# A transformer block with two kinds of attention: the products with the values placed on their own, up to two key tiles in a run

## The chip, the cores and the metric

The kernel runs on one core of a Trainium2 chip. The metric is the device time of one execution in microseconds (us); the lower it is, the better. Engines are named as in the profile: PE is TensorE with its matmuls, PEld its weight loads, DVE is VectorE, ACT is ScalarE, POOL is GpSimd, SP is SyncE, which issues nearly all DMAs here. SBUF is the memory on the core, PSUM the memory that matmuls write, DRAM the memory outside.

## The reference

Eight independent batches of 512 tokens with 256 features pass through four residual layers, all in float32:

```python
x = x + attn_a(layernorm(x))      # 16 heads of 16, latent keys and values, rope, softmax with a distance mask
x = x + ffn(layernorm(x))         # 256 -> 1024, relu, -> 256
x = x + attn_b(layernorm(x))      # one head of 256, no softmax: (q k^T * decay) v
x = x + ffn(layernorm(x))         # the same weights again
# attn_a, cut to its core:
#   q = rope(x Wq + bq);  k, v = split((x Wdown + bdown) Wup + bup);  k = rope(k)
#   att = softmax(q k^T / 4 + mask(distance));   out = att v + 0.2 * sigmoid(q . mean(k)) * mean(v)
#   return out Wo + bo
```

## The kernel before

**The first attention** is cut into items: a batch has four groups of four heads, so there are 32 groups, and a group has eight steps of scores. Score item `n` (`score_item`) holds two heads' scores for one tile of 128 queries against 512 keys; DVE reduces them to row maxima (`reduce_item`, the `mr<-s` of the profile). When a group's eight items are done, the maxima are transposed (`mx`), negated on ACT (`neg`) and sent by a DMA into a spare row of the transposed queries `qT`, so that the second pass of scores comes out with the maximum already subtracted. The second pass (`prob_item`, the `t` of the profile) computes the scores transposed, keys on partitions; ACT takes the exponential into a tile `p` of 128 x 2 x 512 (`soft_item`), and POOL, or DVE where the planner says so, multiplies it by the distance mask, in two halves. The product with the values (`pv_item`) takes two such items, that is four heads and one tile of 128 keys: four matmuls with 32 output columns each, which accumulate over the group's four key tiles into one PSUM bank, `pv`. Each float32 matmul shows as two in the trace. The values carry a column of ones, so that `pv` also holds the sums of the softmax.

After a group's last key tile, the units of `post_units` follow: ACT copies `pv` into `num` (evacuate); then either SP moves `num` into `aT` (numerators, heads on partitions) and `sums`, DVE takes reciprocals, two DMAs spread them through DRAM into `rec`, and DVE divides; or, in groups 2 and 3 of some batches, PE transposes `num` and divides on DVE (`num`, `aT` flips). When a batch's last group is done, `("aT", b)` is given, and the projection `wo` of that batch may begin.

**Everything else** is written as units: layer norms (`st_`, `mv_`, `xn_`, `tr_` for each of the norms a, f, r and g), the latent and rotary fronts (`lat`, `k`, `q`, `v`, `ga`, `me`), `wo`, the hidden layers (`hx`, eight units of four matmuls, then `x`, four units of sixteen), and the second attention (`b`, `bv`, `bs`, `bo`). A unit has an estimated PE time, a list of what other engines do after it, predecessors, and needs.

**The order** on every engine is fixed by the program: the calls are kept in program order, and the function `plan` decides that order. It keeps a clock for each engine and goes through the steps: step `t` issues the scores of item `t` and the second pass of item `t - LAG` (LAG is 12). Between steps it issues units, taking whatever is ready soonest, with a credit that spreads the units over the remaining steps; `posts`, `shifts` and the fronts go ahead of the rest. `plan` is tried with 96 sets of rules, and the set with the lowest planned cost is emitted. After the last step the remaining units follow in the order in which they become ready.

In the kernel before, the values' product belongs to a step. The third entry of a step is `t - LAG - PVLAG` (PVLAG is 3); where that is an odd item, the step begins with one key tile's four matmuls, and then come the scores. Two pairs of banks (`ps_sc`, bufs 2) serve the scores of both passes; three banks (`ps_m`) serve the units; in the early steps the second pass may use those (`spare`). The tiles `p` have four buffers, `num` and `neg` two.

**Loads.** Three buffers hold batches of `x`. The load of batch b + 3 is issued (`fetch`) when the second half of `wo` of batch b has been issued; its DMA then waits, in SP's queue, for DVE's addition that read the old contents. The statistics of the new batch come into DVE's queue from a set step on.

Of the kernel before, what the change touches and what calls it, by code (L numbers as in the profile page):

```python
# [35 lines left out]
def tile_kernel(  # L36
# [47 lines left out]
    ps_m = ctx.enter_context(tc.tile_pool(name="ps_m", bufs=3, space=PSUM))  # L84

    xv = x.rearrange("b (t p) d -> b p t d", p=P)
    ov = out.rearrange("b (t p) d -> b p t d", p=P)
# [32 lines left out]

    wq_in = at.tile([P, NC, NH, 32], F32, tag="p", bufs=4, name="wq_in")

    def load_wq():
        act.dma_start(wq_in.rearrange("p c h d -> p c (h d)"), wq[:, :, 0, :])

    wk_in = at.tile([P, NH, 32], F32, tag="p", bufs=4, name="wk_in")
    move(wk_in.rearrange("p h d -> p (h d)"), wk[:, 0, :].unsqueeze(0).to_broadcast([2, LAT, NH * 32]))
# [126 lines left out]
    NS = 8 * NI  # L254
    LAG, PVLAG = 12, 3
    PER = 8 * NG
# [30 lines left out]
    def bias_rows():  # L287
        move(b_row.rearrange("j (c p) -> p (j c)", p=P), vecs[:, V_BQB : V_BQB + 2 * NC])
        wr["rows"] = at.tile([P, 4, D], F32, tag="p", bufs=4, name="b_rows")
        move(wr["rows"][:, 0:2, :], b_row.unsqueeze(0).to_broadcast([P, 2, D]))  # L290
# [85 lines left out]
    def front1(b):  # L376
# [53 lines left out]
        s, (h0, h1) = ln_units(lambda: xs[b], f"a{b}", fr)  # L430
        free = PER * (b - 1) + LAG + PVLAG + 2
        u = {"lat": Unit(latent, 1720, (("ACT", 700),), after=[h0[2], h1[2]]), "latent": latent}
        u["v"] = Unit(values, 950, (("ACT", 1350),), after=[u["lat"]], step=free, bank=2)
        u["mv"] = Unit(mean_v, 250, (("DVE", 250), ("POOL", 1400)), after=[u["lat"]])
# [14 lines left out]
    def front2(b, u1):  # L449
# [18 lines left out]
        def half_unit(j, e, ps, order="cs"):  # L468
            for n in order:
                table = cos if n == "c" else nsin  # L470
                if b == 0 and (j, e) == (0, 1):
                    if not spare:
                        spare["t"] = at.tile([P, 2, T], F32, tag="p", bufs=4, name="rq1_0")
# [26 lines left out]
        def mean_k():  # L500
            m = fr.tile([P, 2], F32, tag="mk", name=f"mk_{b}")
            for e in range(2):
                unused = fr.tile([P, T], F32, tag="unused", name=f"unused{e}_{b}")
                act.activation(unused, rot[1, e], AF.Identity, accum_out=m[:, e : e + 1])
                gps.tensor_scalar(kmean[:, e, :NH], hmask, m[:, e : e + 1], None, ALU.mult)
# [6 lines left out]

        free = PER * (b - 1) + LAG + PVLAG + 2
        lat = u1["lat"]
# [70 lines left out]
    def soft_item(n, ps):  # L585
        i, r = divmod(n, 8)
        t, pair = r // 2, 1 - r % 2
        p = at.tile([P, 2, T], F32, tag="p", bufs=4, name=f"p_{n}")
        if spare[n]:
            for e in range(2):  # L590
                act.activation(p[:, e, :], ps[e], AF.Exp, scale=0.25)
        else:
            act.activation(p, ps[2], AF.Exp, scale=0.25)
        o = (NT - 1 - t) * P
        eng = gps if pooled[n] else dve
        for e in range(2):
            eng.tensor_tensor(p[:, e, :], p[:, e, :], late["dec_a"][:, o : o + T], ALU.mult)
        probs[(i, t, pair)] = p
# [21 lines left out]
    def post_units_dma(i):  # L620
        b, g = divmod(i, NG)
        c = g // 2

        def evacuate():
            num = at.tile([P, T], F32, tag="num", name=f"num_{i}")
            act.copy(num, pv[i])
            if g == 0:
                aT[b] = at.tile([P, NC, T], F32, tag="aT", name=f"aT_{b}")
            if g % 2 == 0:
                sums[c] = at.tile([P, 2, HD], F32, tag="sums", name=f"sums_{b}_{c}")  # L630
            move(sums[c][:, g % 2, :], num[HD:P:32])
# [13 lines left out]

        def divide():
            dve.tensor_mul(aT[b][:, c, :], aT[b][:, c, :], sums["rows", c])

        u = [Unit(evacuate, then=(("ACT", 600), (None, 7500)))]
        if g % 2:  # L650
            u.append(Unit(invert, then=(("DVE", 350), (None, 12000)), after=u[-1:]))
            u.append(Unit(divide, then=(("DVE", 700),), after=u[-1:], gives=("aT", b) if g == NG - 1 else None))
        return u

    def post_units(i, fast):
# [5 lines left out]
        def evacuate():  # L661
            num = at.tile([P, T], F32, tag="num", name=f"num_{i}")
            act.copy(num, pv[i])
            s["num"] = num
# [29 lines left out]
    def rest(b):  # L694
# [27 lines left out]
        def ffn(norm, src, dst, last):  # L722
# [3 lines left out]
            def up(f):  # L726
                if b == B - 1:
                    if f == 0:
                        s["h"] = []
                    if f % 2 == 0:  # L730
                        s["h"].append(at.tile([P, 2 * T], F32, tag="p", bufs=4, name=f"h_{dst}_{f}"))
                elif f == 0:
# [22 lines left out]
        def keys(o):  # L755
            if o == 0:
                s["v"], s["w"] = [], []
                if b == B - 1:
                    p = [at.tile([P, 2 * T], F32, tag="p", bufs=4, name=f"ret_{j}") for j in range(4)]
                    room = [(p[1], 0), (p[1], D + 1), (p[1], 2 * D + 2), (p[3], 0)]  # L760
# [140 lines left out]
    def plan(reserve, later, early, fast, lead, bias, emit=False):  # L901
# [5 lines left out]
        banks = deque([0, 0, 0])  # L907
        given = {("wo", -2), ("wo", -1), ("x", 1), ("x1", -1)}
# [66 lines left out]

        def values_of(t):
            n = steps[t][2]
            return n if n > 0 and n % 2 == 1 else None

        def step_start(t):  # L980

            s, ts, _ = steps[t]
            n = values_of(t)
            at_ = clock["PE"]
            if n is not None:
                at_ = max(at_, prob_at[n] - 100, prob_at[n - 1] - 100)
            own = 0
# [14 lines left out]
            own = both  # L1002
            return max(at_, own - (1000 if n is not None else 0))

        def step(t):
            s, ts, _ = steps[t]
            at_ = step_start(t)
# [9 lines left out]
            shape[0] = "S"  # L1017
            n = values_of(t)
            if n is not None:
                if emit:  # L1020
                    pv_item(n)
                at_ += 1000
                if n % 8 == 7:
                    us = post_units(n // 8, fast)
                    made = Unit(None)
                    made.done = at_ + 100
                    us[0].after.append(made)
                    posts.extend(us)
            if s is not None or ts:
                at_ += 1070  # L1030
            clock["PE"] = at_
# [45 lines left out]

        gaps, shape, landed = [], ["S"], {}
        shifts, posts = [], []
        setup = [Unit(lambda: xs.update({2: load_x(2)}), step=20, gives=("x", 2))]  # L1080
# [33 lines left out]
        t, credit, share = LAG, 0, 0  # L1114
        while t < LAST or any(chains) or posts or shifts:
            while True:
# [15 lines left out]
            for rank, c in enumerate([shifts, posts] + chains):  # L1132
# [19 lines left out]
            if take and best is None:  # L1152

                able = [c for c in [shifts, posts] + chains if c and c[0].step <= t and start_of(c[0]) is not None]
                if not able:
# [129 lines left out]
```

## Time and profile before

| | |
|---|---|
| time, median of 3 runs | 1297.86 us (1295.99 to 1302.39) |
| the profiled execution | 1296.18 us, span 1294.3 us |
| mean granted TensorE clock | 0.987 |
| matmuls and weight loads in the trace | 6110 each |
| multiplications of `p` by the mask, POOL | 472 halves, 597.5 us |
| the same, DVE | 40 halves, 41.5 us |
| exponentials of 128 x 1024, ACT | 229, mean 1.02 us |

The page of the profile gives busy times by engine, the chain of work that ended last, and groups of instructions (line, engine, operation, names, count, busy time, mean time, and the idle time ahead of them with what ended it). Nearly all instructions stand on two lines, 69 and 201, because helpers issue them; so one goes by names. A name such as `x` can be several tiles (the input, and the results of layers, whose buffer numbers are left out). The trace can be asked for the order of a stretch, for the chain of waits in it and for busy times and granted clock in it.

### The profile page before, as it was taken

The page shows a single profiled execution, that of the slowest core. Times are in us where ns is not written, and L with a number is a line of the kernel's source. Part 1 is how long each engine was busy: PE and PEld are TensorE (multiplying, and loading weights), DVE is VectorE, ACT ScalarE, POOL GpSimd, SP SyncE. Part 2 cuts the span into 40 slices and gives each one's busy share as a digit, 9 for nine tenths or more (in the row PEclk, how much of TensorE's full clock was granted, in tenths as well). Part 3 has the DMA queues.
Part 4 walks back from the last instruction along what each step waited for, and adds up shares of the span by engine and source line. Part 5 has one row for each costly group of instructions (what it writes and reads, how often), then busy time and mean ns, then how long its engine had stood idle before and what let it go on. Part 6 is the DMA issues. An engine that isn't in the chain of part 4 may idle for free.

```text
span 1294.3 us, 15776 instructions
## 1 busy us (share of the span) xinstructions
PE 1235.9 (95%) x6110; PEld 618.5 (48%) x6110; DVE 654.4 (51%) x979; ACT 456.7 (35%) x655; POOL 768.0 (59%) x753
## 2 busy tenths in 40 slices
PE   7999899899999999999999999999999999998998
PEld 5423344244444543445534544445544464575675
DVE  4777665758443675444755267452644354313130
ACT  2245343443434334342243323432343424312201
POOL 4389866787576767765577555783567645602010
PEclk9999999999999999999999989999999999998999
DMA  5301010001000100010000100010000000000000
GB/s 138 126 20 32 9 48 5 10 17 39 9 22 11 45 5 14 5 51 30 14 6 22 38 25 14 6 40 29 12 2 10 18 13 14 1 17 1 1 16 17
DMA packets 30870, 30.80 MB, mean 24 GB/s; under 512 B 12721, under 2 KB 22194, under 8 KB 30516
## 3 DMA queue, kind: packets, MB, share of 16 engines
q1 hardware_dynamic: 29884, 29.01, 8.1%
q8 instruction: 48, 0.79, 0.3%
q10 hardware_dynamic: 912, 0.79, 0.2%
q14 instruction: 26, 0.21, 0.1%
HBM read 13.39 MB, written 4.39 MB: 14 GB/s over the span
## 4 chain that ended last, share of the span: by engine, by line
PE 82%; DVE 12%; DMA 2%; issue 2%; POOL 1%; ACT 1%; SPq 0%; ACTq 0%; DVEq 0%
PE s L201 18%; PE hx L201 17%; PE x L201 17%; DVE mr L69 6%; PE pv L201 5%; PE wo L201 3%; PE bs L201 3%; PE bo L201 3%; PE t L201 2%; PE b L201 2%; PE q L201 2%; PE bv L201 2%; DVE xn_a L69 1%; PE warm L201 1%; PE lat L201 1%
## 5 line engine op out<-in xcount | busy, mean ns | idle before, releaser
L69 POOL TENSOR_TENSOR p<-p,dec_a 128x512 f32<-128x512 f32 x472 | 597.5, 1289 | 265.6 <-ACT p L69 263.2
L69 DVE TENSOR_REDUCE mr<-s 128x2 f32<-128x1024 f32 x256 | 312.5, 1222 | 286.1 <-PE t L201 252.8
L69 ACT ACTIVATE p<-t 128x1024 f32<-128x1024 f32 (+1 forms) x283 | 263.2, 942 | 494.0 <-PE t L201 476.0
L201 PE MATMUL s<-kT,qT 32*128 32x512 f32 x1024 | 290.6, 643 | 26.1 <-DVE mr L69 25.6
L201 PE MATMUL t<-qT,kT 32*128 32x512 f32 x1024 | 290.6, 645 | 2.6 <-DVE mv_a L69 1.6
L201 PE MATMUL x<-w_sb,h_x 128*128 128x256 f32 x1024 | 233.6, 383 | 0.0
L201 PEld LDWEIGHTS x<-w_sb,h_x 128*128 128x128 f32 x1024 | 191.2, 190 | 54.7 <-issue 30.1
L201 PEld LDWEIGHTS s<-kT,qT 32*128 32x128 f32 x1024 | 78.0, 184 | 191.7 <-DVE mr L69 96.3
L201 PE MATMUL pv<-p,va 128*32 128x512 f32 x1024 | 141.6, 619 | 0.0
L69 DVE TENSOR_TENSOR x<-x,x 128x256 f32<-128x256 f32 x64 | 27.2, 424 | 218.9 <-PE x L201 218.9
L69 ACT ACTIVATE h_x<-hx,vec 128x512 f32<-128x512 f32 x128 | 88.0, 687 | 133.2 <-PE hx L201 129.1
L201 PE MATMUL hx<-xT_g,w_sb 128*128 128x512 f32 x256 | 119.5, 614 | 2.0 <-ACT xT_g L69 2.0
L201 PE MATMUL hx<-xT_f,w_sb 128*128 128x512 f32 x256 | 118.7, 602 | 0.8 <-ACT xT_f L69 0.8
L201 PEld LDWEIGHTS t<-qT,kT 32*128 32x128 f32 x1024 | 78.7, 185 | 17.9 <-ACT p L69 5.4
L201 PEld LDWEIGHTS hx<-xT_g,w_sb 128*128 128x128 f32 x256 | 47.8, 195 | 65.6 <-issue 59.1
L201 PEld LDWEIGHTS hx<-xT_f,w_sb 128*128 128x128 f32 x256 | 45.7, 190 | 61.7 <-issue 55.4
L69 POOL TENSOR_TENSOR x<-x,b 128x256 f32<-128x256 f32 x64 | 48.1, 771 | 15.4 <-DVE xn_g L69 8.0
L201 PEld LDWEIGHTS pv<-p,va 128*32 128x32 f32 x1024 | 21.2, 109 | 73.8 <-issue 51.5
L69 POOL TENSOR_SCALAR ve_g<-mv_g 128x2 f32<-128x2 f32 x16 | 3.5, 219 | 85.4 <-DVE mv_g L69 85.4
L69 DVE TENSOR_TENSOR p<-p,dec_a 128x512 f32<-128x512 f32 x40 | 41.5, 1078 | 7.3 <-ACT p L69 7.1
L69 POOL TENSOR_TENSOR rc<-rc,rs 128x512 f32<-128x512 f32 x30 | 39.2, 1329 | 9.1 <-DVE rs L69 9.1
L201 PE MATMUL bs<-xT_r,ret 128*128 128x512 f32 (+3 forms) x128 | 38.3, 441 | 0.0
(144 smaller groups left out, 1068.4 us busy)
## 6 DMA issues: line engine op xcount, KB each, us to landing
kT<-rc SPq DMA_DIRECT2D x64, 64.0 KB
out_dram<-x SPq DMA_DIRECT2D x32, 128.0 KB
qT<-rc SPq DMA_DIRECT2D x60, 64.0 KB
x<-in_x_dram SPq DMA_DIRECT2D x7, 512.0 KB
aT<-num SPq DMA_DIRECT2D x96, 32.0 KB
rec<-d_rec SPq DMA_DIRECT2D x12, 256.0 KB
w_sb<-in_w_dram SPq DMA_DIRECT2D x2, 1024.0 KB
x<-in_x_dram SPq DMA_DIRECT2D x2, 256.0 KB
```

Source lines behind the costliest of these rows:

```text
L69: ins = f(*a, **k)
L201: tc.keep_in_program_order(nc.tensor.matmul(o, lhsT=l, rhs=r, start=start, stop=stop))
```

## The change

The product with the values is taken out of the steps and becomes a thing of its own. A counter `valued[0]` says how many items have been consumed. `values_start(k)` gives the planned time at which the next `k` key tiles (one or two, of the same group) could start: PE's clock, the planned end of the multiplications of their items less 100 ns, and, for a group's first tile, the evacuation of the group before. `values(k)` emits them, and after a group's last tile it makes the units of `post_units`. In the loop, rules decide when: where the buffers of `p` would run out, or after the last step, products go at once (two if the second is soon ready); else two go when both are ready and the last thing issued was a unit, or when the next step is more than 1700 ns away and no unit can start; else one goes when the wait is over 300 ns (FILL) and no unit can start. If a unit could start and the last thing was a step, the unit is issued first. A step thus has only its scores.

The tiles `p` get seven buffers (PB); `num` and `neg` get one each; the mean over the keys writes its unused result into a rotary tile that is no longer needed, in place of a tile of its own. The values' projection of batch b (`u["v"]`) waits for the last product of batch b - 2 by name, where it waited for a step, and the rotary keys' step moves from LAG + PVLAG + 2 to LAG + 1. The 96 sets of rules are as before.

```diff
+    PB = 7
-    LAG, PVLAG = 12, 3
+    LAG, FILL = 12, 300
...
-        free = PER * (b - 1) + LAG + PVLAG + 2
-        u["v"] = Unit(values, 950, (("ACT", 1350),), after=[u["lat"]], step=free, bank=2)
+        u["v"] = Unit(values, 950, (("ACT", 1350),), after=[u["lat"]], needs=(("pv", b - 2),), bank=2)
...
-                unused = fr.tile([P, T], F32, tag="unused", name=f"unused{e}_{b}")
-                act.activation(unused, rot[1, e], AF.Identity, accum_out=m[:, e : e + 1])
+                act.activation(rot["s", 1, e], rot[1, e], AF.Identity, accum_out=m[:, e : e + 1])
...
-        free = PER * (b - 1) + LAG + PVLAG + 2
+        free = PER * (b - 1) + LAG + 1
...
-        neg = at.tile([NG * NT, P], F32, tag="neg", name=f"neg_{i}")
+        neg = at.tile([NG * NT, P], F32, tag="neg", bufs=1, name=f"neg_{i}")
...
-        p = at.tile([P, 2, T], F32, tag="p", bufs=4, name=f"p_{n}")
+        p = at.tile([P, 2, T], F32, tag="p", bufs=PB, name=f"p_{n}")
...
-            num = at.tile([P, T], F32, tag="num", name=f"num_{i}")
+            num = at.tile([P, T], F32, tag="num", bufs=1, name=f"num_{i}")
...
-        steps = [(t, [t - LAG] if t >= LAG else [], t - LAG - PVLAG) for t in range(NS)]
-        steps += [(None, [n, n + 1], n - 3) for n in range(NS - LAG, NS, 2)] + [(None, [], NS - 3), (None, [], NS - 1)]
+        steps = [(t, [t - LAG] if t >= LAG else []) for t in range(NS)]
+        steps += [(None, [n, n + 1]) for n in range(NS - LAG, NS, 2)]
...
+        def values_start(k):
+            d, last = valued[0], valued[0] + 2 * k - 1
+            if d >= NS or d % 8 + 2 * k > 8 or last not in prob_at:
+                return None
+            t = max(clock["PE"], *(prob_at[n] - 100 for n in range(d, last + 1)))
+            return max(t, drawn[0]) if d % 8 == 0 else t
+
+        def values(k):
+            s = values_start(k)
+            stands(s - clock["PE"])
+            clock["PE"] = s + (520 if shape[0] == "S" else 130) + 870 * k
+            shape[0] = "V"
+            for _ in range(k):
+                n = valued[0] = valued[0] + 2
+                if emit:
+                    pv_item(n - 1)
+            if n % 8 == 0:
+                us = post_units(n // 8 - 1, fast)
...
+                posts.extend(us)
+                drawn[0] = max(clock["PE"] + 100, clock["ACT"]) + 700
+                if n % PER == 0:
+                    given.add(("pv", n // PER - 1))
...
-            n = values_of(t)
-            if n is not None:
-                if emit:
-                    pv_item(n)
-                at_ += 1000
-                if n % 8 == 7:
-                    us = post_units(n // 8, fast)
...
+            full = t < LAST and steps[t][1] and steps[t][1][-1] - valued[0] >= PB
+            one, two = values_start(1), values_start(2)
+            soon = clock["PE"] + 50
+            wait = (s_step or clock["PE"] + 2500) - clock["PE"]
+            other = best is not None and best[2] <= soon
+            k = 0
+            if full or t >= LAST and one is not None:
+                k = 2 if two is not None and two <= max(one, clock["PE"]) + 400 else 1
+            elif two is not None and two <= soon and (shape[0] == "U" or wait > 1700 and not other):
+                k = 2
+            elif one is not None and one <= soon and wait > FILL and not other:
+                k = 1
+            if k and other and shape[0] == "S":
+                credit -= best[1][0].pe
+                issue(best[1].pop(0))
+                continue
+            if k and (full or t < LAST or values_start(k) <= soon):
+                values(k)
+                continue
```

More of the change, by code (lines that the diff above doesn't have):

```diff
@@ L119, in tile_kernel @@
     move(bd, vecs[:LAT, V_BD : V_BD + 1].unsqueeze(0).to_broadcast([2, LAT, 1]))
-    wq_in = at.tile([P, NC, NH, 32], F32, tag="p", bufs=4, name="wq_in")
+    wq_in = at.tile([P, NC, NH, 32], F32, tag="p", bufs=PB, name="wq_in")
     def load_wq():
         act.dma_start(wq_in.rearrange("p c h d -> p c (h d)"), wq[:, :, 0, :])
-    wk_in = at.tile([P, NH, 32], F32, tag="p", bufs=4, name="wk_in")
+    wk_in = at.tile([P, NH, 32], F32, tag="p", bufs=PB, name="wk_in")
     move(wk_in.rearrange("p h d -> p (h d)"), wk[:, 0, :].unsqueeze(0).to_broadcast([2, LAT, NH * 32]))
@@ L288, in bias_rows @@
         move(b_row.rearrange("j (c p) -> p (j c)", p=P), vecs[:, V_BQB : V_BQB + 2 * NC])
-        wr["rows"] = at.tile([P, 4, D], F32, tag="p", bufs=4, name="b_rows")
+        wr["rows"] = at.tile([P, 4, D], F32, tag="p", bufs=PB, name="b_rows")
         move(wr["rows"][:, 0:2, :], b_row.unsqueeze(0).to_broadcast([P, 2, D]))
@@ L472, in half_unit @@
                     if not spare:
-                        spare["t"] = at.tile([P, 2, T], F32, tag="p", bufs=4, name="rq1_0")
+                        spare["t"] = at.tile([P, 2, T], F32, tag="p", bufs=PB, name="rq1_0")
                     t = spare["t"][:, "cs".index(n), :]
@@ L661, in evacuate @@
         def evacuate():
-            num = at.tile([P, T], F32, tag="num", name=f"num_{i}")
+            num = at.tile([P, T], F32, tag="num", bufs=1, name=f"num_{i}")
             act.copy(num, pv[i])
@@ L730, in up @@
                     if f % 2 == 0:
-                        s["h"].append(at.tile([P, 2 * T], F32, tag="p", bufs=4, name=f"h_{dst}_{f}"))
+                        s["h"].append(at.tile([P, 2 * T], F32, tag="p", bufs=PB, name=f"h_{dst}_{f}"))
                 elif f == 0:
@@ L758, in keys @@
                 if b == B - 1:
-                    p = [at.tile([P, 2 * T], F32, tag="p", bufs=4, name=f"ret_{j}") for j in range(4)]
+                    p = [at.tile([P, 2 * T], F32, tag="p", bufs=PB, name=f"ret_{j}") for j in range(4)]
                     room = [(p[1], 0), (p[1], D + 1), (p[1], 2 * D + 2), (p[3], 0)]
@@ L907, in plan @@
         banks = deque([0, 0, 0])
-        given = {("wo", -2), ("wo", -1), ("x", 1), ("x1", -1)}
+        given = {("wo", -2), ("wo", -1), ("pv", -2), ("pv", -1), ("x", 1), ("x1", -1)}
         held = []
@@ L974, in shift_unit @@
             return u
-        def values_of(t):
-            n = steps[t][2]
-            return n if n > 0 and n % 2 == 1 else None
+        def values_start(k):
[15 more added lines that the diff above has]
+                us = post_units(n // 8 - 1, fast)
+                made = Unit(None)
+                made.done = clock["PE"] + 100
+                us[0].after.append(made)
+                posts.extend(us)
+                drawn[0] = max(clock["PE"] + 100, clock["ACT"]) + 700
+                if n % PER == 0:
+                    given.add(("pv", n // PER - 1))
         def step_start(t):
-            s, ts, _ = steps[t]
-            n = values_of(t)
+            s, ts = steps[t]
             at_ = clock["PE"]
-            if n is not None:
-                at_ = max(at_, prob_at[n] - 100, prob_at[n - 1] - 100)
             own = 0
@@ L1002, in step_start @@
             own = both
-            return max(at_, own - (1000 if n is not None else 0))
+            return max(at_, own)
         def step(t):
-            s, ts, _ = steps[t]
+            s, ts = steps[t]
             at_ = step_start(t)
@@ L1017, in step @@
             shape[0] = "S"
-            n = values_of(t)
-            if n is not None:
-                if emit:
-                    pv_item(n)
-                at_ += 1000
-                if n % 8 == 7:
-                    us = post_units(n // 8, fast)
[L1025 to L1030, printed above, removed]
+            at_ += 1070
             clock["PE"] = at_
@@ L1078, in plan @@
         gaps, shape, landed = [], ["S"], {}
+        valued, drawn = [0], [0]
         shifts, posts = [], []
@@ L1114, in plan @@
         t, credit, share = LAG, 0, 0
-        while t < LAST or any(chains) or posts or shifts:
+        while t < LAST or any(chains) or posts or shifts or valued[0] < NS:
             while True:
@@ L1152, in plan @@
             if take and best is None:
+                if valued[0] < NS:
+                    values(1)
+                    continue
                 able = [c for c in [shifts, posts] + chains if c and c[0].step <= t and start_of(c[0]) is not None]
```

## The prediction

> **What bounds the kernel now.** I read the page first: busy shares and the chain that ended last.
>
> ```profile
> PE 1235.9 (95%) x6110; PEld 618.5 (48%) x6110; DVE 654.4 (51%) x979; ACT 456.7 (35%) x655; POOL 768.0 (59%) x753
> PE 82%; DVE 12%; DMA 2%; issue 2%; POOL 1%; ACT 1%; SPq 0%; ACTq 0%; DVEq 0%
> ...
> L69 DVE TENSOR_REDUCE mr<-s 128x2 f32<-128x1024 f32 x256 | 312.5, 1222 | 286.1 <-PE t L201 252.8
> L201 PE MATMUL pv<-p,va 128*32 128x512 f32 x1024 | 141.6, 619 | 0.0
> ```
>
> PE has 82% of the chain, DVE 12%. The values' products (`pv`) are 1024 matmuls in 128 key tiles of eight, 141.6 us or 1.1 us a tile. Their number does not change, so the question is what they cost by where they stand. The second view is the timeline of a middle stretch: start, duration, instruction, and in brackets the idle time and its releaser.
>
> ```profile
> 504.39 1.07 PE L201 MATMUL pv<-p,va 128*32 128x512 f32 x8
> ...
> 505.39 0.70 PE L201 MATMUL s<-kT,qT 32*128 32x512 f32 x2
> ...
> 506.46 1.99 PE L201 MATMUL hx<-xT_f,w_sb 128*128 128x512 f32 x4
> ...
> 508.37 0.70 PE L201 MATMUL s<-kT,qT 32*128 32x512 f32 x2
> ...
> 509.44 1.07 PE L201 MATMUL pv<-p,va 128*32 128x512 f32 x8
> 509.55 1.23 DVE L69 TENSOR_REDUCE mr<-s 128x2 f32<-128x1024 f32 x1 [1.76 <-PE t L201]
> ...
> 510.83 0.70 PE L201 MATMUL s<-kT,qT 32*128 32x512 f32 x2 [0.32 <-DVE mr L69]
> ```
>
> Start to start, a tile costs 1.00 us behind a unit (504.39 to 505.39), but 1.39 us straight behind a step (509.44 to 510.83). The step itself is 1.07 us (508.37 to 509.44). The extra 0.39 is a wait: the next step writes scores where the last one's are being reduced, and the reduction (1.23 us) is not done. So two steps start at least 1.07 + 1.39 = 2.46 us apart, and whatever stands between them is free up to that. The third view is the chain of waits around 604 us, with the busy time and granted clock of that stretch and the next (columns PE, PEld, DVE, ACT, POOL, clock, DMA).
>
> ```profile
> 603.64 0.70 DVE x L69
> ...
> 604.36 3.96 DMA x<-in_x_dram
> ...
> 609.32 0.62 DVE xn_r L69 x2
> ...
> 610.81 0.86 DVE mr L69
> ...
> 611.84 2.73 DVE xn_a L69 x2
> ...
> 615.52 1.87 PE pv L201 x8
> ```
> ```profile
> 604.00:622.00 18.00, 15.10 (x64) 5.71 (x57) 13.49 (x26) 5.30 (x7) 10.46 (x15) 0.81 0.09 29
> 622.00:640.00 18.00, 17.84 (x86) 8.08 (x84) 12.47 (x22) 6.55 (x10) 9.13 (x10) 1.00 0.09 25
> ```
>
> Batch 6's input can be loaded only when DVE has added the output projection of batch 3 into the buffer's last reader (603.64). Its statistics stand next in DVE's queue, so DVE stands for the whole load, 4 us, and two reductions, the transposes and the steps are late behind it. PE then runs at 0.81 of its clock. Batch 7 does the same at 760 us.
>
> **The change, part by part.** The scheduler reorders everything, so I took the order in which the changed program lays its instructions on each engine and counted in both orders.
>
> *Shape of the array.* A hidden-layer unit (`hx`, four matmuls) takes 1.717 us between units, 1.821 behind a step, 1.810 ahead of one, 1.914 with both: each change of tile shape costs 0.10 us. A second tile straight behind a first, seen once near the end, started 0.88 us after it, against 1.00. The old order has 582 changes of shape among steps, tiles and the rest. The new one has the 128 tiles in 85 runs (43 pairs) and yet 589 changes, since 60 runs follow a unit, 25 a step, 50 lead into a step and 35 into a unit, and steps now alternate with units more often (step to unit 201 to 222, unit to step 127 to 197). 7 x 0.10 = +0.7 us; three more warming matmuls of 0.21 us add 0.6. Sum +1.3.
>
> [...]
>
> *Steps too close.* I priced what lies between each two steps and took the shortfall to 2.46 us. A lone tile between steps: 52 times, now 10, at 0.39: 20.3 to 3.9. Nothing between them: 9 times, now 15. Without a shape change a step is 0.96 us, so 1.5 each; most old ones lie in the early steps that use spare banks, and there a step followed at once by a step took 2.0 us, which is 0.94 too much. So six more cost 5.6 to 9.0. A short unit (transposes) between: 9.2 to 9.0 us. Sum -16.4 - 0.2 + 5.6 to 9.0, that is -11.0 to -7.6; I take -8, since the new direct neighbours include eight later steps that have no spare banks.
>
> *The loads of batches 6 and 7.* From the second half of the projection of batch b-3 (its `wo`) to the first transposes of batch b there were 9 us of PE work for b = 6 and 7, 16 for 5 and 22 for 4. In the new order these are 39, 37, 50 and 46. Against that stand 4 us of load and about 7 of statistics and normalizing (608.35 to 614.56), so the wait should go entirely. What it cost: from 605.61 to 620.42 PE ran eight things (`ga`, `mv`, `tr_r`, step, `tr_a`, tile, step, `me`) that cost 1.91 + 0.53 + 0.44 + 1.07 + 0.59 + 1.00 + 1.07 + 0.97 = 7.6 us elsewhere; they took 14.8, 7.2 too many. The same eight from 760.87 to 774.81 took 13.9, 6.3 too many. Sum -13.5, the half clock included. Next late there is nothing of DMA; DVE's own queue bounds, as in other batches.
>
> *The queues that products are moved past.* With a group's last tile goes its evacuation (ACT), then five DMAs of SP per group, the reciprocal, two more DMAs and the division. In the old trace, batches 3 to 6 needed 27 to 29 us from the last tile's start to the division's end, with the projection long after it. Now the projection stands 23.4, 32.9, 32.9 and 23.0 us of PE work behind the last tile, and in batch 0 only 3.0. The old evacuation began nearly 3 us after the tile's end, because exponentials stood ahead of it on ACT; the new order puts it first, and the reciprocal and division had slack (the broadcast of the reciprocals was issued at 1005.3, the division ran at 1019.5). Lower bound 0, upper 4 + 5 us for batches 3 and 6 and some 8 for batch 0. I take +1.5. On SP, kT's eight DMAs (6 us of issue) now stand ahead of the last group's sums in batches 4 and 5; 33 us cover that.
>
> *Probabilities.* A product waits for POOL's two multiplications: 4.9 us after its step's start in the median, 5.9 in nine of ten. With PE work and the 2.46 us alone, 12 tiles now come within 6 us of that step, the closest at 4.5; 0 to +3 us, I take +0.5. Seven buffers keep ACT's exponentials from waiting. POOL gives 3 of its 236 tiles to DVE (2.2 us each), and DVE is busy 51%: nothing. One buffer fewer of `num` and `neg`, and the sum of keys written into a dead tile: old holders are done by 20 us; nothing.
>
> *Start and tail.* The prologue is unchanged, and from the last flip of batch 7 (`num_31`) on both orders are the same, so their waits stay. Another wait, 313 to 323 us (PE busy 7.5 of 10, clock 0.83), falls in a region that is reordered: 0 to -4, taken as 0.
>
> Sum: +1.3 - 8 - 13.5 + 1.5 + 0.5 = -18.2. The profiled execution took 1296.18 us (span 1294.3), so 1278.0; the median of runs is 1.7 above it: 1279.7, say 1279.5.
>
> [...]
>
> **The rivals.** *The projection waits (slower).* Batches 0, 2, 3 and 6 are the place. If the chain behind the last tile keeps its old length (11 us through flips in batch 0, 28 by DMA), `wo` stands at PE's head for 8 + 3.4 + 4.6 + 5 = 21 us, and each stand is followed by 3.4 to 6.8 us at half clock, 4 x 1.7 to 3.4 = 7 to 14. In place of my +1.5 that gives -19.7 + 21 + 10 = +11: 1309. It decides once these four waits exceed 20 us with their clock. Against it: the early evacuation and the slack above. 0.10.
>
> *The loads' gain does not come* (same). The projection moved ahead, but SP's queue is in order, and x_6 and x_7 stand behind qT's DMAs and output stores that wait for POOL and DVE; or the late reductions return behind other DVE work. Then only -4.7 is left: 1293. 37 us of distance speak against it. 0.10.
>
> *The runs do not do what they say.* Shape changes do not fall, so the pairs alone give +0.7; with a load gain that is already in my sum.
>
> **How the numbers follow.** Forecast (both gains) 0.80; its own range takes all lower bounds (+1.3 - 11 - 13.5 - 4 = -27, 1271) to the upper ones with one load's wait left (+1.3 - 7.6 - 6.3 + 6 = -6.6, 1291). Half of the second rival (up to 1296) belongs in the range, the first stays out: 1269 to 1296. About 0.5% (6.5 us) is what a measurement of this kernel tells from no change: faster 0.79, same 0.10, slower 0.11.
>
> **What would show it.** Right: no wait of `st_a` for the load of `x`, half-clock windows gone at both places; waits of `s` for `mr` down by some 8 us; `pv` total near 128 x 1.1 less 43 x 0.1. Wrong: `wo` or aT waiting long after a group's end, PE waiting for `p` of POOL by more than 5 us in all, or new half-clock slices in the middle.

## The result and the profile after

The changed kernel takes 1283.9 us (median; 1283.1 to 1288.7), the one before 1297.86 us. The ratio is 0.9895, interval 0.987 to 0.992: 14 us less, 4.4 us short of the forecast. The profiled execution took 1283.11 us, its span 1281.3, so the two profiled spans differ by 13.0 us.

The page after, in the rows that answer to those of before (the last number of a row is the idle time of the engine ahead of the group, and what ended it):

```profile
PE 1227.7 (96%) x6116; PEld 617.3 (48%) x6116; DVE 662.6 (52%) x985; ACT 459.9 (36%) x654; POOL 760.1 (59%) x747
PE 88%; DVE 7%; DMA 1%; issue 1%; POOL 1%; ACT 1%; SPq 0%; DVEq 0%; ACTq 0%
...
L69 DVE TENSOR_REDUCE mr<-s 128x2 f32<-128x1024 f32 x256 | 312.3, 1222 | 287.0 <-PE t L203 265.1
L203 PE MATMUL s<-kT,qT 32*128 32x512 f32 x1024 | 291.7, 644 | 19.8 <-DVE mr L69 19.7
L203 PE MATMUL pv<-p,va 128*32 128x512 f32 x1024 | 129.2, 605 | 0.0
```

DVE's share of the chain that ended last fell from 12 to 7% and PE's rose from 82 to 88%. DVE has no less work than before; PE waits for it less. The products with the values fell from 141.6 to 129.2 us of busy time, 12.4, where 43 pairs at 0.1 would have given 4.3. That row is not a price, because the busy times of neighbours overlap (a pair of tiles in the changed kernel begins at 587.32 and is busy for 1.92 us, to 589.24, while the next entry begins at 589.17); the work as a whole, priced below, did not fall.

The waits before and after (engine, who waited for what: us in total, times, longest):

```profile
PEld s L201 <- DVE mr L69: 96.3, 87, 2.8
...
PEld pv L201 <- POOL p L69: 17.0, 27, 1.2
...
DVE st_a L69 <- DMA x<-in_x_dram: 8.3, 3, 4.0
```
```profile
PEld s L203 <- DVE mr L69: 70.5, 71, 2.8
...
PEld pv L203 <- POOL p L69: 11.2, 20, 1.5
...
DVE st_a L69 <- DMA x<-in_x_dram: 0.7, 1, 0.7
```

The first is the room between two steps, the second POOL's multiplications, the third the statistics of a new batch standing for its load. These rows of the weight loads are no prices either: PE itself stood 25.6 us for the reductions before and 19.7 after, 5.9 less. The load of batch 7 in the kernel before, then, in the changed kernel, the stretches at the times of those two loads and three others (columns: busy us of PE, PEld, DVE, ACT, POOL, then granted clock):

```profile
760.00:775.00 15.00, 13.18 (x53) 5.01 (x51) 11.57 (x22) 4.71 (x6) 9.54 (x14) 0.77 0.12 35
```
```profile
570.00:590.00 20.00, 14.56 (x82) 7.70 (x75) 10.16 (x18) 4.37 (x6) 8.60 (x10) 0.91 0.13 28
605.00:622.00 17.00, 17.00 (x91) 9.64 (x90) 9.48 (x17) 4.74 (x6) 10.38 (x10) 1.00 0.01 1
760.00:775.00 15.00, 15.00 (x84) 7.99 (x83) 11.50 (x26) 4.83 (x6) 9.57 (x12) 1.00 0.00 1
1160.00:1172.00 12.00, 7.84 (x19) 3.73 (x20) 6.31 (x21) 2.45 (x4) 8.58 (x14) 0.72 0.00 1
1240.00:1256.00 16.00, 12.82 (x37) 7.19 (x36) 2.94 (x10) 2.60 (x5) 3.95 (x6) 0.79 0.05 18
```

At 605 and 760 us, where PE stood for a while and ran at 0.81 and 0.77 of its clock, it is now busy without a break at full clock. A new low row stands at 570 to 590 us. Of the two in the tail, the kernel before had the first too (at 1179 us).

To see where the 13 us went I gave every PE entry of both orders the price that its shape usually has in the traces, plus 0.1 us per change of shape, and took the rest of each stretch as time above the work:

| stretch (score steps) | before: us, of it above the work | after: us, of it above the work |
|---|---|---|
| start to 63 | 226.0, 34.1 | 232.3, 34.2 |
| 64 to 95 | 125.7, 13.8 | 127.5, 7.9 |
| 96 to 127 | 132.5, 5.1 | 140.5, 3.3 |
| 128 to 159 (load of batch 6) | 143.4, 13.3 | 144.6, 10.7 |
| 160 to 191 (load of batch 7) | 154.4, 10.3 | 145.6, 4.3 |
| 192 to 254 | 307.1, 10.9 | 299.5, 11.1 |
| 255 to the end | 197.3, 17.0 | 183.2, 18.3 |
| sum | 1286.4, 104.5 | 1273.2, 89.8 |

The duration of a stretch alone says little, because the planner moved units from one to another; the second number is what counts. It fell by 14.7, and the work rose by 1.5. The stretch with batch 7's load gained 6.0, the one with batch 6's load only 2.6: something new stands there.

That is at 577 us. PE and DVE of the changed kernel (start, duration, instruction, idle time ahead and its releaser):

```profile
576.90 0.70 PE L203 MATMUL wo<-wo_sb,aT 128*128 128x256 f32 x2
581.00 1.22 PE L203 MATMUL wo<-wo_sb,aT 128*128 128x256 f32 x2 [3.40 <-DVE aT L69]
```
```profile
577.00 1.23 DVE L69 TENSOR_REDUCE mr<-s 128x2 f32<-128x1024 f32 x1 [1.23 <-PE t L203]
578.18 2.16 DVE L69 TENSOR_TENSOR p<-p,dec_a 128x512 f32<-128x512 f32 x2
580.27 0.68 DVE L69 TENSOR_TENSOR aT<-aT,rec 128x512 f32<-128x512 f32 x1
```

The projection of batch 3 reaches PE's head at 576.9 and stands, because the division that completes `aT` runs only at 580.27, behind a reduction and a multiplication of probabilities that were queued on DVE ahead of it. By the prices this projection takes 5.0 us too long: 3.4 of standing, and 1.7 because PE ran at half its clock from 580.4 to 583.8 us. The projections of batches 6 and 0 stand 1.2 and 0.9. The planner allows it: `("aT", b)` is given when the division has been issued, and nothing in the projection's start time asks when it will be done.

### The profile page after: what moved, and what is told of

Read it like the earlier page. It is cut to its first block, busy times and chain, and to the rows that moved or that the text cites. A ratio compares the mean times of both kernels' runs of the same rounds, so it can differ in the third digit from the quotient of the medians.

```text
span 1281.3 us, 15818 instructions
## 1 busy us (share of the span) xinstructions
PE 1227.7 (96%) x6116; PEld 617.3 (48%) x6116; DVE 662.6 (52%) x985; ACT 459.9 (36%) x654; POOL 760.1 (59%) x747
## 4 chain that ended last, share of the span: by engine, by line
PE 88%; DVE 7%; DMA 1%; issue 1%; POOL 1%; ACT 1%; SPq 0%; DVEq 0%; ACTq 0%
PE s L203 19%; PE x L203 18%; PE hx L203 18%; PE pv L203 8%; PE wo L203 3%; PE bs L203 3%; PE bo L203 3%; DVE mr L69 3%; PE b L203 2%; PE bv L203 2%; PE q L203 2%; PE t L203 2%; PE warm L203 1%; DMA wv_sb<-in_wv_dram 1%; PE lat L203 1%
## 5 line engine op out<-in xcount | busy, mean ns | idle before, releaser
L69 POOL TENSOR_TENSOR p<-p,dec_a 128x512 f32<-128x512 f32 x466 | 588.5, 1287 | 278.4 <-ACT p L69 278.2
L203 PE MATMUL s<-kT,qT 32*128 32x512 f32 x1024 | 291.7, 644 | 19.8 <-DVE mr L69 19.7
L203 PE MATMUL pv<-p,va 128*32 128x512 f32 x1024 | 129.2, 605 | 0.0
L203 PE MATMUL hx<-xT_g,w_sb 128*128 128x512 f32 x256 | 126.5, 628 | 1.3 <-ACT xT_g L69 1.3
L203 PEld LDWEIGHTS pv<-p,va 128*32 128x32 f32 x1024 | 24.9, 109 | 74.6 <-issue 53.3
L69 DVE TENSOR_TENSOR p<-p,dec_a 128x512 f32<-128x512 f32 x46 | 45.1, 1018 | 19.6 <-ACT p L69 19.6
L203 PE MATMUL wo<-wo_sb,aT 128*128 128x256 f32 x128 | 35.5, 395 | 5.2 <-DVE aT L69 4.3
```

Of the source, the lines that this page charges most:

```text
L69: ins = f(*a, **k)
L203: tc.keep_in_program_order(nc.tensor.matmul(o, lhsT=l, rhs=r, start=start, stop=stop))
```

## The experiments

My theory before them: two things gained (steps further apart, loads of `x` covered), and the projection's wait and the half clock took part of it back. The rivals: the gain is a matter of buffers, or of pairs alone. Each ratio is to the kernel before; "against the changed kernel" is the difference of the ratios times 1297.86.

### A fourth buffer for x, in the kernel before

```diff
-    xp = ctx.enter_context(tc.tile_pool(name="xp", bufs=3))
+    xp = ctx.enter_context(tc.tile_pool(name="xp", bufs=4))
```

Nothing else is changed, and the order stays as it was.

> The kernel before with four buffers of x in place of three, and every engine's instructions in the same order: the load of batches 6 and 7 no longer waits for the addition of batch 3 and 4. Theory (most of the gain is the two waits of DVE's statistics for these loads, 7.2 + 6.3 us of PE time): 1297.9 - 13.5 = 1284.4, at least 11 us faster, no wait of st_a for the load at 604 and 760 us. Rival (the gain comes from the runs of products and the wait would be covered anyway): 1297.9, within 3 us.

Measured: 1290.7 us, ratio 0.9927 (0.9903 to 0.9951), 9.5 us less, where I expected at least 11. The statistics wait 0.9 us in all for a load, in place of 8.3. The windows of the two places:

```profile
604.00:622.00 18.00, 17.18 (x89) 8.12 (x90) 15.76 (x28) 7.01 (x9) 13.93 (x19) 1.00 0.02 4
...
760.00:776.00 16.00, 15.19 (x81) 7.06 (x79) 14.13 (x19) 7.10 (x11) 10.73 (x14) 1.00 0.04 9
```

Steps 128 to 159 went from 143.4 to 137.2 us, steps 160 to 191 from 154.4 to 149.1: together 11.5, of which 6.8 is the half clock (two windows of 6.8 us at half rate; the rows of the kernel before have 0.81 of the clock over 18 us and 0.77 over 15). So the term was real and about 2 us smaller than the 13.5 predicted; in both places PE still has about 0.8 us of idle time. The span shows only 3.8 less than before, because in this execution half-clock windows came in or grew longer in the prologue, the early steps and the tail, where not one instruction was moved: without the two windows its mean clock is still 0.986, against 0.987.

### The reduction in two halves, in both kernels

```diff
-        dve.tensor_reduce(
-            mrow[i % 2][:, 2 * pair : 2 * pair + 2, t], ps, AX.X, ALU.max
-        )
+        for e in range(2):
+            dve.tensor_reduce(
+                mrow[i % 2][:, 2 * pair + e : 2 * pair + e + 1, t], ps[:, e : e + 1, :], AX.X, ALU.max
+            )
```

This lengthens DVE's part of every step by a little, and so counts the places in which a step waits for it. In the kernel before:

> The kernel before with each reduction of 128 x 1024 done as two of 128 x 512, same order else, same result. By the other instructions of 512 columns a half takes some 0.7 us, so a pair takes 0.15 to 0.25 us longer than the 1.22 of one. Theory (a step that follows too close waits for the reduction): the 75 places of the old order that fall short of 2.46 us between steps each grow by that, +11 to +19 us: 1309 to 1317. Rival (the 0.39 us behind a product is the array's change of shape or the exponential): no change, 1298, since DVE is busy 51%.

and in the changed kernel:

> The changed kernel with the same split of each reduction. Theory: only 41 places fall short of 2.46 us, so +6 to +10 us: 1290 to 1294, and the distance between the two kernels grows from 14 to 19 to 23 us. Rival (both kernels wait for DVE's total load alike): both grow by the same amount, the distance stays 14.

The group's row, before and after the change:

```profile
L69 DVE TENSOR_REDUCE mr<-s 128x1 f32<-128x512 f32 x512 | 328.2, 683 | 286.0 <-PE t L201 251.9
```
```profile
L69 DVE TENSOR_REDUCE mr<-s 128x1 f32<-128x512 f32 x512 | 328.2, 683 | 279.9 <-PE t L203 259.6
```

Two halves take 2 x 0.683 = 1.366 us in place of 1.222, 0.144 more. The kernel before became 12.5 us slower (1312.3 us, ratio 1.0096, 1.0073 to 1.0119). The changed one took 1288.3 us, ratio 0.991 (0.9887 to 0.9934): 2 us above the changed kernel by the ratios (the intervals overlap), 5.0 by the profiled spans, which were 15.0 apart for the kernel before. By the order, 75 pairs of steps were short of 2.46 us before and 41 are now; times 0.144 that is 10.8 and 5.9. The 12.5 fits the first; the second came out below its count and below the 6 to 10 expected; and the distance between the two kernels grew from 14 to 24 us, a little over what was expected. So the changed order is much less tied to the reduction, and the count of short pairs gives the direction and the rough size.

### Never two tiles in a run

```diff
-            one, two = values_start(1), values_start(2)
+            one, two = values_start(1), None
```

> The changed kernel with the rules for two key tiles in a run taken out, so that products go one at a time by the same other rules (five chance pairs of runs remain). The order has 631 changes of shape against 589 (+4.2 us at 0.10 each) and a shortfall between steps of 29.8 us against 35.6 (-5.9). Theory (runs of two are worth next to nothing, what counts is that products leave the steps): 1283.9 - 1.7 = 1282, between 1278 and 1287. [...]

Measured: 1287.6 us, ratio 0.9912 (0.9883 to 0.9941), 2.2 us above the changed kernel, with intervals that overlap, at the upper end of what was expected. Eight pairs remain by the trace, not five. The order now has 631 changes of shape in place of 589, +4.2 us, but its shortfall between steps is 29.8 in place of 35.6. If each of 43 pairs saved two changes of shape at the 0.10 us measured, taking the pairs out would cost some 8.6 us; the rise is far below that. Whether they are worth 2 us or nothing stays open.

### The projection waits for the division in the plan

```diff
+                if n % PER == 0:
+                    first_wo[n // PER - 1].after.append(us[-1])
```

(`first_wo[b]` is the first unit of that batch's projection; `us[-1]` is the division.)

> The changed kernel whose planner lets a batch's projection start only when the last division (or copy) of that batch is done by its clock; before, the projection became ready as soon as the division had been issued. The order shifts: projections stand 24 to 27 us of PE work behind the last product, the shortfall between steps is 38.3 us against 35.6. Theory (what the prediction mis-sized is this wait: 5.0 us at batch 3, 1.2 at batch 6, 0.9 at batch 0, and 1.7 us of half clock behind it): 1283.9 - 8.8 + 2.7 = 1278, between 1275 and 1281, no wait of wo for aT over 1.5 us. Rival (the DMAs are the wait and come back at another place): 1284.

Measured: 1293.8 us, ratio 0.9951 (0.993 to 0.9972), 7 us slower than the changed kernel. The wait for `aT` at batch 3 was gone, as meant. But a changed due time moves everything behind it: by the prices this order spends 102.1 us above the work, where the changed kernel spends 89.8; nine lone transposes now stand between two steps, three in the changed kernel, and around one of them the steps start 3.76 us apart (880.14 and 883.90). My expectation fell as a whole: it took the rest of the order as given (and its 8.8 us counted the 1.7 of half clock twice, as the 5.0 holds them). The run shows that 5 us at one place are easily lost in the draw of a new order; it does not show what the wait itself costs.

### Four buffers of probabilities

```diff
-    PB = 7
+    PB = 4
```

> The changed kernel with four buffers of p (PB = 4), so that the rule for full buffers forces products sooner. The order has 653 changes of shape against 589 (+6.6 us), a shortfall between steps of 39.0 us against 35.6 (+3.4), and 22 products within 6 us of their step against 12 (+1 to +5). Theory (the buffers bring the freedom of place): 1283.9 + 13 = 1297, between 1292 and 1301, so nearly all of the gain is gone, although the loads of batches 6 and 7 still come early. Rival (the gain is the early loads alone, buffers add nothing): 1284 to 1287.

Measured: 1313.8 us, ratio 1.0091 (1.0062 to 1.0121): slower than the kernel before, and 25 us above the changed one, twice what was expected. The loads were still early. The order has 653 changes of shape, and the products go where a buffer must be freed, not where there is room; by the prices the work grew by 8.8 us and the time above it by 19.5. The projection of batch 6 now does what that of batch 3 did:

```profile
1039.31 0.70 PE L203 MATMUL wo<-wo_sb,aT 128*128 128x256 f32 x2
1043.33 0.70 PE L203 MATMUL wo<-wo_sb,aT 128*128 128x256 f32 x2 [3.32 <-DVE aT L69]
```

This too is a new order, so the run gives the price of four buffers with these rules in one draw; how much of it a luckier order would save is open.

### Seven buffers in the kernel before

```diff
-        p = at.tile([P, 2, T], F32, tag="p", bufs=4, name=f"p_{n}")
+        p = at.tile([P, 2, T], F32, tag="p", bufs=7, name=f"p_{n}")
```

> The kernel before with seven buffers of probabilities in place of four (room made by single buffers of num and neg and the dead rotary tile); the order on every engine stays. Theory: buffers alone do nothing, because in the kernel before ACT's exponentials wait for PE's second pass (476 us of idle time) and never for a buffer; what the buffers buy is the freedom of the order. 0 us, ratio 0.998 to 1.001. Rival: with more buffers exponentials and POOL run further ahead and the 17 us in which products wait for POOL shrink: -5 to -10 us, ratio 0.992 to 0.996; then a part of what the change gained would be due to the buffers alone.

Measured: 1301.0 us, ratio 1.001 (0.9989 to 1.0031). Buffers alone do nothing for the time. What the rival said of the wait did come true: the weight loads of the products wait 11.9 us for POOL in place of 17.0, almost as little as after the change (11.2). It bought no time, so that wait was not what held the kernel. With the run before this one: the rules need the buffers, and the buffers need the rules.

### The small edits alone, in the kernel before

```diff
-        neg = at.tile([NG * NT, P], F32, tag="neg", name=f"neg_{i}")
+        neg = at.tile([NG * NT, P], F32, tag="neg", bufs=1, name=f"neg_{i}")
```

The same for `num`, and the dead rotary tile for the mean over the keys.

> The kernel before with one buffer each of num and neg and with the sum of the keys written into the dead rotary tile: the small parts of the change alone, order the same. Theory (nothing waits for them): 1298, within 3 us. Rival (the evacuation of a group waits for the DMAs of the one before): 1303 or more.

Measured: 1299.0 us, ratio 0.9993 (0.997 to 1.0016). Nothing, as costed. Two more parts of the change, the earlier step of the rotary keys and the new condition of the values' projection, were not tried by themselves.

### Warming matmuls in the gaps of the tail

```diff
+                gap = best[2] - clock["PE"]
+                if t >= LAST and gap > 700 and banks[0] <= clock["PE"]:
+                    n = min(20, (gap - 300) // 218)
+                    banks.popleft()
+                    banks.append(clock["PE"] + n * 218)
+                    if emit:
+                        warm(n)
```

Behind the last step of the changed kernel, 27 matmuls of the identity go into eight planned gaps.

> The changed kernel with warming matmuls (128 x 128 of the identity into a free bank) in the gaps that the planner sees after the last step, 27 in eight places, nothing else moved. Theory (the trace after has two stretches of 6.8 us at half clock in the tail, at 1164 and 1246 us, which cost 3.4 us each, and they follow from PE standing idle): 1283.9 - 3.4 to 6.8 = 1277 to 1280.5, and no half clock after 1150 us. Rival (the half clock follows something else, or the warming matmuls themselves are late): 1284 to 1289.

Measured: 1282.1 us, ratio 0.9852 (0.9821 to 0.9884), 5.6 us below the changed kernel, though the intervals (0.987 to 0.992 there) just overlap; so the trace has to carry it. There the half-clock window at 1164 us is gone and the one at 1246 us is 3.4 us long in place of 6.8; the tail is 3.2 us shorter. I expected no half clock after 1150 us, and some is left. The median lies above the range expected; the ratio times 1297.86 is 1278.7, within it.

### The division of batch 3 with less in front of it

```diff
-        eng = gps if pooled[n] else dve
+        eng = gps if pooled[n] or n == 135 else dve
```

> The changed kernel with one multiplication of probabilities (that of item 135, 2.16 us on DVE at 578.2) given to POOL; every other instruction keeps its place. Theory: the 5.0 us that PE stands for the division of batch 3 came of DVE's queue: ahead of the division stand a reduction to 578.2 and this multiplication to 580.3. Without it the division starts at about 578.2 and ends at 578.9, so PE's wait falls from 5.0 to about 2.9 us. With the half clock that followed (580.4 to 583.8, 1.7 us lost) gone or not, the time is 2 to 4 us below the changed kernel's: ratio to the kernel before 0.986 to 0.988. Rival 1: the division waited for its DMAs (the broadcast of the reciprocals, issued at 565.5), not for DVE: the wait stays at 5 us and the ratio at 0.9895. Rival 2: POOL, which multiplies another tile until 579.2, hands item 135 over only at 581.7, and the product of that item, eight PE entries behind the projection, waits instead: part of the gain comes back, 0 to -1 us.

Measured: 1282.6 us, ratio 0.9874 (0.9846 to 0.9903), 2.7 us below the changed kernel, with overlapping intervals; so the stretch decides. Its PE, DVE and POOL:

```profile
579.27 0.70 PE L203 MATMUL wo<-wo_sb,aT 128*128 128x256 f32 x2
582.15 1.16 PE L203 MATMUL wo<-wo_sb,aT 128*128 128x256 f32 x2 [2.19 <-DVE aT L69]
```
```profile
579.37 1.23 DVE L69 TENSOR_REDUCE mr<-s 128x2 f32<-128x1024 f32 x1 [1.23 <-PE t L203]
580.51 1.58 DVE L69 TENSOR_TENSOR aT<-aT,rec 128x512 f32<-128x512 f32 x1
```
```profile
579.07 4.16 POOL L69 TENSOR_TENSOR p<-p,dec_a 128x512 f32<-128x512 f32 x3
```

The one of these that runs when the division begins, by itself:

```profile
580.29 1.26 POOL L69 TENSOR_TENSOR p<-p,dec_a 128x512 f32<-128x512 f32 x1
```

The division begins 1.24 us after PE has reached the projection, where it was 3.37: 2.13 sooner, about the length of the multiplication that was taken away, and right behind the reduction. So it was DVE's queue that held it, not the DMAs. Nor does a product wait behind the projection, as the second rival had it. But the division now takes 1.58 us in place of 0.68, and the projection is 4.1 us too long in place of 5.0: half of what was expected, and the half clock behind it stayed, with its 1.7 us in both figures. What differs is POOL: in the changed kernel it was idle during the division (its multiplication ended at 579.2), here it multiplies throughout.

The rows show when the division ended: 0.55 us after the multiplication of POOL that was running when it began (580.29 + 1.26 + 0.55 = 582.10), 0.9 us later than a division of 0.68 us would have. The other profiles have the same. Of the 156 divisions in all 13 of them, 48 began while POOL had more than 0.2 us left of multiplying or adding tiles of 256 or 512 columns; each ended 0.55 us after that instruction of POOL (0.546 to 0.552), and so took 0.78 to 1.78 us (1.60 at 562.08 in the kernel before, 1.58 at 866.18 in the changed one). The other 108 took 0.68 to 0.72, also where POOL began only after them. What ties the two engines together no run shows.

### Both together

> The changed kernel with item 135 on POOL and with warming matmuls in the gaps of the tail. Theory: the two are in different stretches (580 us and 1160 to 1256 us), so they add: -5.5 for the warming as measured alone, -2 to -4 for the wait, 7.5 to 9.5 us below the changed kernel, ratio 0.982 to 0.984, about 1275 to 1277 us. Rival: which stalls bring the half clock is not fixed; then the sum falls short and the ratio stays at 0.985.

Measured: 1278.7 us, ratio 0.9837 (0.981 to 0.9865), 7.5 us below the changed kernel, where the two alone add to 8.3. The tail's windows:

```profile
1160.00:1172.00 12.00, 9.96 (x45) 6.04 (x44) 4.51 (x14) 3.18 (x7) 7.22 (x13) 1.00 0.01 2
1240.00:1256.00 16.00, 14.16 (x43) 6.90 (x42) 1.32 (x6) 5.01 (x8) 2.44 (x4) 1.00 0.02 8
```

Full clock at both places, and from step 255 to the end it takes 4.9 us less than the changed kernel. The window at 580 us stayed. This version beats both kernels, and its interval lies clear of that of the changed kernel.

## Why the prediction was right, and where its sum was off

*Steps too close, -8.* Right. Counted with the same prices in both orders the shortfall went from 43.1 to 35.6, -7.5; no run measures this term by itself, but PE's own wait for the reductions fell by 5.9 us (some 8 were named), and the reduction in halves shows on the chip that the new order depends less on it. Part of this fell in steps 64 to 95.

*Loads of batches 6 and 7, -13.5.* Right in mechanism and place; 11.5 by the fourth buffer. What was a little off is the step that charged all time beyond the usual cost of the eight things to the load: with the load early, PE still waits 0.8 us in each place.

*Shape of the array, +1.3.* By the prices the work rose by 1.5. The sign is what matters: pairs save changes of shape, and the new order spends them again (589 changes, 582 before).

*The queues that products are moved past, +1.5.* This step failed, in size. The bounds were 0 and 4 + 5 us for batches 3 and 6 and some 8 for batch 0, and I took a value near the lower one, because evacuation, reciprocal and DMAs had slack. In the changed order they did. What I had not counted is DVE's own queue ahead of the division: 23 us of PE work lie between the group's last tile and the projection, and the division still came last, behind a reduction that waited for a step of its own and a multiplication placed there by the planner. The time lost at the projections rose from 1.8 us (batch 0 before) to 7.1, in which the 1.7 for the half clock at 580 to 584 us are counted: +5.3, in place of +1.5. The run with item 135 on POOL shows the cause: without the multiplication the division began 2.13 us sooner. The slow rival thus had the right place and less than a quarter of its 31 us: one long stand and not four. Batch 0, where I put 8, got better.

*The wait at 313 to 323 us, 0 to -4, taken as 0.* It went: both half-clock windows of steps 64 to 95 (244 and 319 us, 3.4 us lost) are absent after. They are absent too in the three runs that keep the changed kernel's order of work and its reductions, and each of the four runs that keep the old order has one or two in those steps. Why is not shown.

*Probabilities, +0.5; start and tail, 0.* Waits of products for POOL fell (17.0 to 11.2), which by the run with seven buffers alone is worth nothing that shows. In the tail the order is the same and so are the stalls, but time above the work rose by 1.3 us, and there a second stall was followed by the half clock.

Sum of what was found: +1.5 - 7.5 - 11.5 + 5.3 - 3.4 + 1.3 = -14.3, against -13.2 in the table; 1.1 us stays unexplained. The predicted -18.2 was off by the projection (3.8 us), the loads (2) and the tail (1.3), with the 313 us wait (3.4) in the other direction. That wait had been put at nothing, so it was partly luck that the forecast missed by 4.4 us and no more. Of the signs named as wrong, two came true in small: `wo` waiting long once, and a new half-clock slice in the middle. A third, PE waiting for `p` of POOL by more than 5 us, holds for the weight loads (11.2), but they had waited 17.0 before, so it could not tell right from wrong.

## What to carry to other kernels

When work is taken out of a fixed step and placed by itself, follow what its completion releases through every queue up to the engine that finishes it: the slack of the DMAs in between says nothing about the reduction and the multiplication already queued on that engine. Freedom to place work pays only with the buffers that carry it: seven buffers without the rules gave nothing, the rules with four were slower than the kernel before. A planner's order is a draw: repairing one wait by a changed due time cost 7 us in all, whereas an edit that left the order alone could be read. Small stalls in a part that nothing covers can be worth filling with dummy matmuls: here that brought the tail back to full clock in one place, at 5.6 us less by the ratios, and, with the other edit, in both (a clock of 1.00, where the changed kernel had 0.72 and 0.79).

## What the runs showed of the hardware

The half clock (a granted clock of 0.5) mostly comes in windows of 3.4 us (four in the kernel before, two in the changed one) or of twice that (three in each); two of the runs on the kernel before, seven buffers and the small edits, have one of three times that, 10.2 us. The same stalls do not always bring it. Two stalls of the tail, the longest about 2.6 us by the prices, stand in both kernels. Windows around them in the kernel before, and in that kernel with the fourth buffer:

```profile
1174.00:1188.00 14.00, 9.42 (x27) 4.94 (x26) 6.96 (x21) 2.44 (x4) 8.57 (x14) 0.76 0.00 0
1256.00:1270.00 14.00, 10.82 (x37) 6.19 (x36) 2.66 (x9) 3.23 (x5) 3.95 (x6) 1.00 0.06 20
```
```profile
1170.00:1182.00 12.00, 8.27 (x22) 3.85 (x20) 5.12 (x17) 2.62 (x5) 7.82 (x14) 0.72 0.00 0
1252.00:1264.00 12.00, 8.82 (x20) 4.02 (x19) 2.04 (x7) 2.47 (x4) 2.44 (x4) 0.72 0.04 12
```

The second stall ran at full clock in one and was followed by half clock in the other. This is most of the spread between executions: those of the changed kernel had spans of 1281.3 us at a mean clock of 0.989 and 1286.9 at 0.984, and 0.005 of 1284 us is 6.4. A single profiled span can therefore hide several us of gain, as with the fourth buffer, and the place has to be compared, not the span.

Most stalls ahead of these windows are shorter than 3.4 us. In the two kernels none of them but the first of the kernel before and the projection's 3.4 us is over 2.7 us by the prices; ahead of the window at 612.8 to 619.6 us in the kernel before, the longest idle time of PE between 602 us and its start is 1.64 us.

The other surprise is the division of 0.68 us that took 1.58 us with POOL multiplying when it began. Moving work from DVE to POOL gave back 0.9 of the 2.1 us that it freed.
